# One RGCN highway layer on Trainium2: three pairs of blocks of h transposed by DMA, the edge index begun earlier on 16-bit keys

## The chip, the cores and the metric

The kernel runs on one core of a Trainium2 chip. The metric is the device time of one execution in microseconds. Before the change it was 1338.72 us (median of three runs, 1337.65 to 1338.93).

## What is computed

`x` has 1250 rows of 1024 numbers, there are 20000 edges (`src`, `dst`) of 8 types. The layer normalises the rows, lets h gather from its neighbours by type, and mixes the result with h by a gate:

```python
def _rgcn(x, edge_index, edge_type, weight, root, bias):
    msgs = x[src]
    out = x @ root + bias
    for r in range(weight.shape[0]):
        mask = (edge_type == r).astype(x.dtype)
        sums = jax.ops.segment_sum(msgs * mask[:, None], dst, num_segments=n)
        cnt = jax.ops.segment_sum(mask, dst, num_segments=n)
        mean = sums / jnp.maximum(cnt, 1.0)[:, None]
        out = out + mean @ weight[r]
    return out
...
h = jnp.maximum(_layernorm(x, axis=-1), 0.0)
u = _rgcn(h, edge_index, edge_type, weight, root, bias)
z = jnp.concatenate([u, h], axis=1) @ w_gate + b_gate
return x + jnp.tanh(u) * z + h * (1.0 - z)
```

Everything is float32; all weights are 1024x1024 (`w_gate` is two such).

## The kernel before

**Matrices and pairs.** h is multiplied with eleven 1024x1024 matrices in turn: the eight of the edge types, `root`, and the two halves of `w_gate`, the last of them with u. Matrix one is the first of them (`s == 0`). The ten blocks of 128 rows (the last has 98) are taken as five pairs, counted from zero: pair i is block i beside block i + 5. A pair times a matrix is a two-by-two scheme with seven products (Strassen-Winograd; `product`), each 128x512 by 512x512: `p1` (A11), `p5` (S1), the sixth (S2), `p3` (S4), `p7` (S3), `p2` (A12), the fourth (A22). One `lead` bank of PSUM collects several of them and is copied out by ScalarE in between, so a product that goes on adding into a bank waits for the copy before it. From matrix two on, some products are themselves divided (`First`, `Second`, `Third`).

**Where the operands come from.** For each pair `h_op[i]` holds seven operands, with h transposed: A11, A12, A21 and A22 are the transposed quarters, S1 to S4 are sums of them (`left`, on VectorE). A block of h is 128 rows by 1024; `transposed` (L366) has TensorE turn eight 128x128 pieces of it into two PSUM banks, ScalarE copies one bank out and VectorE the other. This happens once, beside matrix one: `norms` (L1220) normalises block after block (statistics on VectorE, root and relu on ScalarE), stores h and x + h to DRAM, and calls `factored` for the pair, then `left`.

**The order.** It is written by hand: each engine does its instructions in the order in which the program issues them. After each product, `between(j)` is called, one *call*; what stands beside the products is written as generators that go one step on at each call. In matrix one, pair i, these are calls 7i to 7i + 6. `index` (L1269) runs `norms` and `columns` (keys of the edges, as columns) side by side, and after both `slots`: for 40 groups of four chunks of 128 edges it works out at which place of `table` each edge goes. A group goes through a round of two calls, in several stages: one-hots on ScalarE (L1055 to L1057), counts on TensorE (L1069), sums on VectorE, a look on TensorE (L1124), place and rank on VectorE (L1132 to L1145). Keys and their low seven bits were written to DRAM as 32-bit words and are read again, broadcast over the partitions, group by group (`load_keys`, L1088). After every four rounds `to_table` issues the 16 scatters of those edges on GpSimd (L1163). `order` then sorts nodes by their number of edges. When it is done, `beside_group` (L1462) follows with `passes_over` (two small reads of maxima) and the counts.

**Queues.** SyncE (SP) issues loads of x, the stores of h and x + h (L874, L880), of the results y (L592), and the loads of keys, in program order; ScalarE issues most loads of weights; GpSimd the scatters and gathers.

**Memory.** x and its statistics live in `xpool`, which was closed with the last pair's operands, when `slots` opened its own pool in the same place.

Of the kernel before, what the change touches and what calls it, by code (L numbers as in the profile page):

```python
# [9 lines left out]
F32 = mybir.dt.float32  # L10
BF16 = mybir.dt.bfloat16
I32 = mybir.dt.int32
AF = mybir.ActivationFunctionType
# [6 lines left out]
def tile_rgcn_highway(  # L20
# [74 lines left out]
    def nedges(c):  # L95
        return P if c < NCH - 1 else EL
# [14 lines left out]
    keys_dram = dram.tile([NCH * P], I32, name="keys_dram")  # L111
    los_dram = dram.tile([NCH * P], I32, name="los_dram")
# [251 lines left out]
    def transposed(aop, part, of, n, relu=False):  # L364


        for half, to in enumerate(((A11, A12), (A21, A22))[part]):
            p = bank().rearrange("p (k f) -> p k f", k=KQ)
            for i in range(KQ):
                k = KQ * half + i  # L370
                nc.tensor.transpose(p[:, i, :n], of[:n, k * P:(k + 1) * P], ident[:n, :n])
            to_n, p_n = aop[:, to, :, :n], p[:, :, :n]
            if half and relu:
                nc.vector.tensor_scalar_max(to_n, p_n, 0.0)
            elif half:
                nc.vector.tensor_copy(to_n, p_n)
            else:
                nc.scalar.activation(to_n, p_n, AF.Relu if relu else AF.Copy)
            if n < P:
                nc.gpsimd.memset(aop[:, to, :, n:], 0.0)  # L380
# [426 lines left out]
    room = [keep.tile([P, 2, n], F32, name=f"inner{k}") for k, n in enumerate((H, H, P, P))]  # L807
    p5_room = keep.tile([P, H], F32, name="inner4")

    with ExitStack() as early:  # L810
        ix1 = early.enter_context(tc.tile_pool(name="ix1", bufs=1))


        first_part = early.enter_context(ExitStack())
        xpool = first_part.enter_context(tc.tile_pool(name="xpool", bufs=3))
# [159 lines left out]
        def columns():  # L975
# [18 lines left out]
            for to, of in ((keys_dram, key_i), (los_dram, lo_i)):  # L994
                nc.sync.dma_start(to[:P * P].rearrange("(c p) -> c p", p=P), of[:, 0, :])
                nc.sync.dma_start(to[P * P:].rearrange("(c p) -> c p", p=P), of[:C2, 1, :])
# [5 lines left out]
            for g in range(1, G):  # L1002
                less = late
                nc.vector.tensor_scalar(less, f["typ"], float(R0[g]),
                                        float((R0[g - 1] - R0[g]) * N),
                                        op0=OP.is_ge, op1=OP.mult)
                nc.vector.tensor_add(row, row, less)
            yield
# [24 lines left out]
            yield  # L1033

        def slots(ix):
# [115 lines left out]
            def to_table(c0, c1):  # L1151
# [9 lines left out]
                for c in range(c0, c1):  # L1161
                    n = nedges(c)
                    ins = nc.gpsimd.indirect_dma_start(  # L1163
                        out=table[:, :],
                        out_offset=bass.IndirectOffsetOnAxis(ap=at_i[:n, c:c + 1], axis=0),
                        in_=row_col[:n, c:c + 1], in_offset=None,
                        bounds_check=G * KEYS * SLOTS - 1, oob_is_err=False)
                    tc.declare_no_dep(ins.ins, query=no_wait, group="scatter", reason="each edge has its own slot")
                    tc.add_to_no_dep_group("scatter", ins.ins)

            load_keys(0)
            for j in range(ng + 3):
                for f, of in ((one_hots, j), (load_keys, j + 1), (as_bf16, j - 2),
# [45 lines left out]

        def norms():  # L1220
# [27 lines left out]
            left(h_op[2])  # L1248
            x4 = [load_x(4, 0)]
            yield  # L1250
            yield
# [39 lines left out]
        todo = index()  # L1291
# [15 lines left out]
    with ExitStack() as edges_part:  # L1307
# [154 lines left out]
        def beside_group():  # L1462

            yield
            passes_over()
# [343 lines left out]
```

## Time and profile before

The profile shows one execution of 1337.41 us; its span, from the first to the last instruction, is 1335.6 us.

| | us |
|---|---|
| median of the runs | 1338.72 |
| profiled execution | 1337.41 |
| its span | 1335.6 |
| TensorE busy | 1323.3 |
| VectorE busy | 956.9 |
| GpSimd busy | 568.5 |
| ScalarE busy | 372.7 |
| 72 + 8 transposes of h (L371), records of 274 and 248 ns | 9.8 |
| 157 scatters of edges (L1163), each | 1.05 |

Busy time is the time in which an engine had an instruction under way; records of TensorE overlap, so the length of one is more than its distance from the next. Each 128x512 product of four matmuls shows as eight records, two for each matmul. In a row of the order of time stand start, length, engine, line, operation, what is written and read, the shape and how many; an idle time before it and what ended it stand in brackets. A line with "q" (ACTq, SPq) is the queue of an engine issuing a DMA.

### The profile page before, as it was taken

What the parts mean: (1) busy time and instruction counts of PE and PEld (TensorE: products, weight loads), DVE (VectorE), ACT (ScalarE), POOL (GpSimd) and SP (SyncE); (2) the same over time, 40 slices, a digit from 0 to 9 for tenths busy, and PEclk for the clock granted to TensorE, in tenths of its full rate; (3) what the DMA queues carried; (4) which work ended last, traced back from release to release, by engine and by line L of the source; (5) the groups of instructions that cost most, each with busy time, mean ns of one, the idle gap of its engine ahead of it and who ended that gap; (6) DMA issues with size and microseconds to landing.
All of it is one profiled execution on the core that took longest, in us unless ns stands there. A gap on an engine that the chain in (4) does not pass through costs nothing.

```text
span 1335.6 us, 13410 instructions
## 1 busy us (share of the span) xinstructions
PE 1323.3 (99%) x4168; PEld 722.1 (54%) x4168; DVE 956.9 (72%) x1823; ACT 372.7 (28%) x794; POOL 568.5 (43%) x509
## 2 busy tenths in 40 slices
PE   9999999999999999999999999999999999999997
PEld 5444555455455545655655565565556556544443
DVE  7753755674675467448987978897778889867875
ACT  3335556465641212111121121112121112221210
POOL 0000364554657036501454546346365555615631
PEclk9999999999999999999999999999999999999999
DMA  8745476866754241143738778878788957969961
GB/s 318 270 182 175 104 124 141 191 126 109 172 160 95 88 114 53 53 148 111 254 127 319 244 253 333 290 238 268 277 273 301 347 192 243 308 251 296 340 168 59
DMA packets 104319, 270.94 MB, mean 203 GB/s; under 512 B 20100, under 2 KB 22354, under 8 KB 104112
## 3 DMA queue, kind: packets, MB, share of 16 engines
q1 hardware_dynamic: 44048, 119.85, 29.3%
q0 software_dynamic: 44064, 118.20, 27.7%
q10 hardware_dynamic: 16128, 31.98, 7.7%
q8 instruction: 33, 0.54, 0.2%
q14 instruction: 46, 0.38, 0.1%
HBM read 212.63 MB, written 75.49 MB: 216 GB/s over the span
## 4 chain that ended last, share of the span: by engine, by line
PE 85%; issue 4%; DVE 2%; DMA 2%; POOL 1%; ACT 0%; POOLq 0%; DVEq 0%; ACTq 0%
PE ps_b L406 41%; PE ps L406 17%; PE ps L219 14%; PE ps_b L219 4%; PE ps_n L406 4%; PE ps_q L219 2%; PE ps_n L219 2%; PE ps_q L406 2%; DMA w<-in_L_gnn_b_gate_dram 1%; DMA h_op<-z_dram,node 1%; POOL out_dram L746 1%; DVE row L1733 0%; DVE row L1734 0%; PE ps_q L1069 0%; PE ps_q L1124 0%
## 5 line engine op out<-in xcount | busy, mean ns | idle before, releaser
L406 PE MATMUL ps_b<-w,h_op 128*128 128x512 f32 x1464 | 659.6, 595 | 1.0 <-ACT row L489 0.8
L406 PEld LDWEIGHTS ps_b<-w,h_op 128*128 128x128 f32 x1464 | 273.6, 190 | 308.4 <-issue 297.4
L1339 POOL DMA_INDIRECT got<-y,idx x193 | 245.8, 1274 | 290.3 <-DVE u L1344 184.1
L1344 DVE SCALAR_TENSOR_TENSOR u<-got,w_of,u 128x1024 f32<-128x1024 f32 (+1 forms) x193 | 246.9, 1282 | 31.8 <-DMA got<-y,idx 29.3
L406 PE MATMUL ps<-w,h_op 128*128 128x512 f32 (+1 forms) x592 | 264.8, 589 | 0.1
L1163 POOL DMA_INDIRECT table<-row_col,at_i x157 | 165.2, 1052 | 185.5 <-DVE at_i L1159 133.0
L406 PEld LDWEIGHTS ps<-w,h_op 128*128 128x128 f32 x592 | 111.0, 190 | 119.2 <-issue 115.0
L431 DVE TENSOR_TENSOR row<-row 128x512 f32<-128x512 f32 x44 | 30.3, 690 | 79.0 <-ACT row L430 79.0
L430 ACT COPY row<-ps_b 128x512 f32<-128x512 f32 x53 | 31.1, 586 | 194.1 <-PE ps_b L406 194.1
L406 PE MATMUL ps_n<-w,h_op 128*128 128x512 f32 x176 | 80.1, 592 | 0.0
L489 ACT COPY row<-ps_b 128x512 f32<-128x512 f32 x54 | 31.7, 586 | 163.6 <-PE ps_b L406 163.4
L219 PE MATMUL ps<-w,h_op 128*128 128x256 f32 x288 | 74.5, 381 | 0.0
L219 PE MATMUL ps<-w,w 128*128 128x256 f32 x288 | 71.1, 380 | 0.0
L529 ACT COPY row<-ps_b 128x512 f32<-128x512 f32 x40 | 23.4, 585 | 162.6 <-PE ps_b L406 142.3
L219 PEld LDWEIGHTS ps<-w,h_op 128*128 128x128 f32 x288 | 54.0, 190 | 27.1 <-issue 21.6
L219 PE MATMUL ps<-inner,inner 128*128 128x256 f32 x264 | 67.8, 379 | 0.0
L219 PEld LDWEIGHTS ps<-w,w 128*128 128x128 f32 x288 | 54.6, 190 | 21.8 <-issue 15.8
L219 PEld LDWEIGHTS ps<-inner,inner 128*128 128x128 f32 x264 | 50.2, 190 | 14.5 <-issue 8.4
L1145 DVE SCALAR_TENSOR_TENSOR junk<-k_bc,key_col,before 128x128 f32<-128x128 int32 x157 | 55.0, 350 | 4.2
L406 PEld LDWEIGHTS ps_n<-w,h_op 128*128 128x128 f32 x176 | 33.4, 190 | 39.5 <-issue 39.0
L457 ACT COPY row<-ps_b 128x512 f32<-128x512 f32 x54 | 31.7, 587 | 75.9 <-PE ps_b L406 71.3
L1055 ACT ACTIVATE is_lo<-io,less_lo 128x128 bf16<-128x128 f32 x157 | 50.1, 391 | 0.7 <-DMA xh_dram<-xt 0.7
(238 smaller groups left out, 1469.5 us busy)
## 6 DMA issues: line engine op xcount, KB each, us to landing
y<-row SPq DMA_DIRECT2D x72, 512.0 KB
w<-in_L_gnn_weight_dram ACTq DMA_DIRECT2D x21, 1024.0 KB
w<-in_L_gnn_weight_dram SPq DMA_DIRECT2D x10, 1024.0 KB
k_bc<-keys_dram SPq DMA_DIRECT2D x39, 256.0 KB
l_bc<-los_dram SPq DMA_DIRECT2D x39, 256.0 KB
w<-in_L_gnn_w_gate_dram ACTq DMA_DIRECT2D x6, 1024.0 KB
h_dram<-h_op SPq DMA_DIRECT2D x9, 512.0 KB
u<-in_L_gnn_bias_dram SPq DMA_DIRECT2D x9, 512.0 KB
```

The source lines that it names most:

```text
L219: nc.tensor.matmul(p, a[:, k, :], b[:, k, :], start=(fresh and k == 0), stop=(k == 1), skip_group_check=True)
L406: nc.tensor.matmul(b[:, at], aop[:, i, k, :], w.of[i][:, k, at], start=(fresh and k == 0), stop=(k == KQ - 1), skip_group_check=True)
L430: nc.scalar.copy(d, b)
L431: nc.vector.tensor_add(c22, c if lone else c22, d)
L457: nc.scalar.copy(c11, b)
L489: nc.scalar.copy(c12, b)
L529: nc.scalar.copy(c21, b)
L1055: nc.scalar.activation(is_lo[:, i, :], io, AF.Abs, bias=less_lo[:, c0 + i:c0 + i + 1])
L1145: nc.vector.scalar_tensor_tensor(junk, o["k_bc"][:, i, :], key_col[:, c:c + 1], before, op0=OP.is_equal, op1=OP.mult, accum_out=rank[:, c: ...
L1163: ins = nc.gpsimd.indirect_dma_start(out=table[:, :], out_offset=bass.IndirectOffsetOnAxis(ap=at_i[:n, c:c + 1], axis=0), in_=row_col[:n, ...
L1339: nc.gpsimd.indirect_dma_start(out=t[:n], out_offset=None, in_=y[g][:, :], in_offset=bass.IndirectOffsetOnAxis(ap=at[:n, d, k:k + 1], axis=0),
L1344: nc.vector.scalar_tensor_tensor(u[:n], t[:n], w, u[:n], op0=OP.mult, op1=OP.add)
```

## The change

The transposes of pairs two, three and four of h leave TensorE. `in_halves` has ScalarE copy a block of h into two halves, all low 16-bit words and then all high ones; `turned` has SP issue one DMA that transposes the block of 128x2048 16-bit words; `whole_again` puts low and high words together again in `h_op`, one quarter on ScalarE and one on VectorE. `turn` does this for the two blocks of a pair, a step at a time: two steps that cut and send, two that put together. The buffers are parts of `h_op[3]` and `h_op[4]` that are not yet in use, and `room_all`, which is one tile now. Pairs zero and one stay with `transposed`.

`norms_and_index` lets `columns`, `slots` and `order` run on during `norms`, but for the calls that `norms` marks HEAVY; so the index begins eleven calls sooner. `xpool` therefore stays open, and the keys are 16 bits wide, in DRAM and in the buffers. `columns` has one more rest. Scatters of edges go into a list, of which two are issued at each rest of a round. `beside_group` waits for call one of pair two.

```diff
-    keys_dram = dram.tile([NCH * P], I32, name="keys_dram")
-    los_dram = dram.tile([NCH * P], I32, name="los_dram")
+    keys_dram = dram.tile([NCH * P], I16, name="keys_dram")
+    los_dram = dram.tile([NCH * P], I16, name="los_dram")
...
+    def in_halves(of, n, to):
+
+        if n < P:
+            nc.gpsimd.memset(to[n // 32 * 32:], 0.0)
+        nc.scalar.copy(to.bitcast(U16)[:n].rearrange("p (h c) -> p h c", h=2),
+                       of.bitcast(U16)[:n].rearrange("p (c h) -> p h c", h=2))
+
+    def turned(of, to):
+
+        nc.sync.dma_start_transpose(to.bitcast(U16).rearrange("p (c r) -> p c r", r=P),
+                                    of.bitcast(U16))
+
+    def whole_again(aop, part, of, n):
+
+        of = of.bitcast(U16).rearrange("p (h a k r) -> p h a k r", h=2, a=2, r=P)
+        for a, to in enumerate(((A11, A12), (A21, A22))[part]):
+            (nc.vector.tensor_copy if a else nc.scalar.copy)(
+                aop[:, to].bitcast(U16).rearrange("p k (r h) -> p h k r", h=2)[..., :n],
+                of[:, :, a, :, :n])
...
+    room_all = keep.tile([P, 4 * H + 4 * P], F32, name="inner")
+    room = [room_all[:, a:a + 2 * n].rearrange("p (k n) -> p k n", k=2)
+            for a, n in ((0, H), (2 * H, H), (4 * H, P), (4 * H + 2 * P, P))]
...
+        xpool = early.enter_context(tc.tile_pool(name="xpool", bufs=3))
         first_part = early.enter_context(ExitStack())
-        xpool = first_part.enter_context(tc.tile_pool(name="xpool", bufs=3))
...
-            for to, of in ((keys_dram, key_i), (los_dram, lo_i)):
+            for to, of, name in ((keys_dram, key_i, "key_h"), (los_dram, lo_i, "lo_h")):
+                half = ix0.tile([P, 2, P], I16, name=name)
+                nc.vector.tensor_copy(half, of)
+                of = half
...
+        placed = []
+
+        def scatter(count):
+
+            for c in placed[:count]:
+                n = nedges(c)
+                ins = nc.gpsimd.indirect_dma_start(
+                    out=table[:, :],
+                    out_offset=bass.IndirectOffsetOnAxis(ap=at_i[:n, c:c + 1], axis=0),
+                    in_=row_col[:n, c:c + 1], in_offset=None,
+                    bounds_check=G * KEYS * SLOTS - 1, oob_is_err=False)
+                tc.declare_no_dep(ins.ins, query=no_wait, group="scatter", reason="each edge has its own slot")
+                tc.add_to_no_dep_group("scatter", ins.ins)
+            del placed[:count]
...
                 for name, of, bufs in (("k_bc", keys_dram, 5), ("l_bc", los_dram, 3)):
-                    t = now.setdefault(j, {})[name] = ix.tile([P, CG, P], I32, name=name,
+                    t = now.setdefault(j, {})[name] = ix.tile([P, CG, P], I16, name=name,
                                                               bufs=bufs)
                     nc.sync.dma_start(t[:, :m, :].rearrange("p c e -> p (c e)"),
                                       of[None, c0 * P:(c0 + m) * P].to_broadcast([P, m * P]))
...
-                for c in range(c0, c1):
-                    n = nedges(c)
-                    ins = nc.gpsimd.indirect_dma_start(
-                        out=table[:, :],
-                        out_offset=bass.IndirectOffsetOnAxis(ap=at_i[:n, c:c + 1], axis=0),
-                        in_=row_col[:n, c:c + 1], in_offset=None,
-                        bounds_check=G * KEYS * SLOTS - 1, oob_is_err=False)
-                    tc.declare_no_dep(ins.ins, query=no_wait, group="scatter", reason="each edge has its own slot")
-                    tc.add_to_no_dep_group("scatter", ins.ins)
+                placed.extend(range(c0, c1))
...
+                        scatter(CG // 2)
                         yield
                     elif 0 <= of < ng:
                         f(of)
...
                 for _ in range(7):
+                    scatter(CG // 2)
                     yield
+                scatter(len(placed))
...
+        def turn(i, blocks, second, *of):
+
+            def flat(t):
+                return t.rearrange("p a k f -> p (a k f)")
+
+            to, of = (room_all[:, :D], flat(second)), [flat(t) for t in of]
+            for part in range(2):
+                b = blocks[part]
+                in_halves(b.ht, b.n, of[part])
+                turned(of[part], to[part])
+                yield
+            for part in range(2):
+                whole_again(h_op[i], part, to[part], blocks[part].n)
+                yield
+
         def norms():
             for _ in range(3):
                 yield
             x3 = [load_x(3, part) for part in range(2)]
             b2 = [Normed(2 + part * NP, x2[part], scratch(NP - 1, part)) for part in range(2)]
             both(*b2)
-            yield
+            for b in b1:
+                b.with_x()
+            yield
+            turn_of = turn(2, b2, h_op[3][:, 0:2], h_op[3][:, S2:S3 + 1], h_op[4][:, S2:S3 + 1])
+            next(turn_of)
             for b in b2:
                 b.store()
             yield
-            for b in b1:
-                b.with_x()
-            yield
-            factored(2, b2)
+            next(turn_of)
+            yield
             b2[0].with_x(b2[0].ht)
             b2[1].with_x()
+            x4 = [load_x(4, 0)]
+            yield
+            next(turn_of)
+            yield
+            next(turn_of)
+            yield
             left(h_op[2])
-            x4 = [load_x(4, 0)]
-            yield
             yield
             b3 = [Normed(3 + part * NP, x3[part], scratch(NP - 1, part)) for part in range(2)]
             both(*b3)
-            yield
+            yield HEAVY
+            turn_of = turn(3, b3, h_op[3][:, S1:S2 + 1], h_op[4][:, S2:S3 + 1], h_op[3][:, 0:2])
+            next(turn_of)
             for b in b3:
                 b.store()
-            yield
-            factored(3, b3)
-            left(h_op[3])
+            yield HEAVY
+            next(turn_of)
             yield
             for b in b3:
                 b.with_x()
             x4.append(load_x(4, 1))
             yield
+            next(turn_of)
+            yield
+            next(turn_of)
+            yield
+            left(h_op[3])
+            yield
+            b4 = [None, None]
+            turn_of = turn(4, b4, h_op[4][:, S1:S2 + 1], h_op[4][:, 0:2], h_op[4][:, S3:S4 + 1])
             for part in range(2):
-                ht = xpool.tile([P, D], F32, name="xt") if part else scratch(NP - 1, 1)
-                b = Normed(4 + part * NP, x4[part], ht)
+                ht = xpool.tile([P, D], F32, name="xt") if part else \
+                    h_op[4][:, S3:S4 + 1].rearrange("p a k f -> p (a k f)")
+                if part:
+                    b4[0].with_x()
+                b = b4[part] = Normed(4 + part * NP, x4[part], ht)
                 b.stats(0)
                 b.stats(1)
                 b.spread()
                 b.relu()
                 b.store()
                 yield
-                yield
-                transposed(h_op[4], part, b.ht, b.n)
-                b.with_x()
-                yield
+                next(turn_of)
+                yield HEAVY
+            b4[1].with_x()
+            next(turn_of)
+            yield
+            next(turn_of)
+            yield
             left(h_op[4])
+
+        def index():
+            yield from columns()
             first_part.close()
-
-        def index():
-            for _ in zip_longest(norms(), columns()):
-                yield
             with tc.tile_pool(name="ix", bufs=2) as ix:
                 yield from slots(ix)
             for k, t in enumerate((key_col, row_col.bitcast(F32), rank)):
                 nc.sync.dma_start(edges_dram[k], t)
             yield from order()
 
-        todo = index()
+        def norms_and_index():
+
+            later = index()
+            for heavy in norms():
+                if not heavy:
+                    next(later)
+                yield
+            yield from later
+
+        todo = norms_and_index()
         going = [True]
 
         while going[0]:
         def beside_group():
 
             yield
+            while at_call != [2, 1]:
+                yield
             passes_over()
```

More of the change, by code (lines that the diff above doesn't have):

```diff
@@ L12 @@
 I32 = mybir.dt.int32
+I16 = mybir.dt.int16
+U16 = mybir.dt.uint16
 AF = mybir.ActivationFunctionType
@@ L378, in transposed @@
                 nc.scalar.activation(to_n, p_n, AF.Relu if relu else AF.Copy)
+            if n < P:
+                nc.gpsimd.memset(aop[:, to, :, n:], 0.0)
+    def in_halves(of, n, to):
+        if n < P:
+            nc.gpsimd.memset(to[n // 32 * 32:], 0.0)
[10 more added lines that the diff above has]
+                of[:, :, a, :, :n])
             if n < P:
@@ L805, in rows_and_weights @@
                 yield
-    room = [keep.tile([P, 2, n], F32, name=f"inner{k}") for k, n in enumerate((H, H, P, P))]
+    room_all = keep.tile([P, 4 * H + 4 * P], F32, name="inner")
+    room = [room_all[:, a:a + 2 * n].rearrange("p (k n) -> p k n", k=2)
+            for a, n in ((0, H), (2 * H, H), (4 * H, P), (4 * H + 2 * P, P))]
     p5_room = keep.tile([P, H], F32, name="inner4")
@@ L1218, in order @@
                     yield
+        HEAVY = True
+        def turn(i, blocks, second, *of):
[10 more added lines that the diff above has]
+                yield
         def norms():
@@ L1241, in norms @@
             yield
-            for b in b1:
-                b.with_x()
+            next(turn_of)
             yield
-            factored(2, b2)
             b2[0].with_x(b2[0].ht)
             b2[1].with_x()
-            left(h_op[2])
             x4 = [load_x(4, 0)]
             yield
+            next(turn_of)
+            yield
+            next(turn_of)
+            yield
+            left(h_op[2])
             yield
```

## The prediction

> **What bounds the kernel now.** I read the page's busy shares first, then TensorE's order of time through matrix one, then ScalarE's, SyncE's and the busy time by stretch for the same microseconds.
>
> ```profile
> span 1335.6 us, 13410 instructions
> ...
> PE 1323.3 (99%) x4168; PEld 722.1 (54%) x4168; DVE 956.9 (72%) x1823; ACT 372.7 (28%) x794; POOL 568.5 (43%) x509
> ...
> PEclk9999999999999999999999999999999999999999
> ...
> q0 software_dynamic: 44064, 118.20, 27.7%
> ```
>
> TensorE is idle for 12.3 of 1335.6 us, and the granted clock is full in every slice. So only two things can move the time: matmul work taken off TensorE, and new waits of TensorE. Next, TensorE in order of time (start, length, instructions):
>
> ```profile
> 42.16 3.60 PE L406 MATMUL ps_b<-w,h_op 128*128 128x512 f32 x8
> ...
> 46.40 3.70 PE L406 MATMUL ps<-w,h_op 128*128 128x512 f32 x8
> 49.94 1.91 PE L371 MATMUL ps<-ident,h_op 128*128 128x128 f32 x16
> 51.69 3.60 PE L406 MATMUL ps_b<-w,h_op 128*128 128x512 f32 x8
> ...
> 65.42 1.91 PE L371 MATMUL ps<-ident,h_op 128*128 128x128 f32 x16
> 67.39 3.70 PE L406 MATMUL ps<-w,h_op 128*128 128x512 f32 x8
> ...
> 81.22 1.04 PE L371 MATMUL ps<-ident,h_op 128*128 128x128 f32 x8
> 82.10 3.60 PE L406 MATMUL ps<-w,h_op 128*128 128x512 f32 x8
> ...
> 92.40 0.84 PE L371 MATMUL ps<-ident,xt 98*128 98x98 f32 x8
> 93.08 3.62 PE L406 MATMUL ps<-w,h_op 128*128 128x512 f32 x8
> ```
>
> One product is eight records and takes 3.43 us from start to start (42.16 to 45.59). The transposes stand in this row with nothing beside them: what follows starts when they are through, so their price is the distance of starts.
>
> **The change, part by part.**
>
> *Taken off TensorE.* The transposes of pairs two, three and four (counting from zero): 51.69-49.94 = 1.75, 67.39-65.42 = 1.97, 82.10-81.22 = 0.88, 93.08-92.40 = 0.68, together **5.28 us**. Nothing is added to TensorE: its counts, looks and products are the same instructions, and the two transposes of `passes_over` stay in their place, because the new gate (pair two, call one of matrix five) is where the old order already had them. With them go six PSUM copies on ScalarE (0.60) and six on VectorE (0.69), neither of which set TensorE's pace.
>
> *Added on ScalarE.* Six deinterleaves (`in_halves`, 128x2048 of two bytes) and six of the copies of `whole_again`. The rows to price them:
>
> ```profile
> 13.16 1.06 ACT L952 ACTIVATE h_op<-h_op 128x1024 f32<-128x1024 f32 x1
> ...
> 45.08 0.57 ACT L469 COPY row<-ps 128x512 f32<-128x512 f32 x1
> 45.80 0.59 ACT L489 COPY row<-ps_b 128x512 f32<-128x512 f32 x1
> ```
>
> 512 more elements cost 1.06-0.59 = 0.47, so 2048 cost 2.47-0.47 = 2.0 us if elements count, 1.06 if bytes do; I take 2.0, since no row shows a copy faster per element. A half of `whole_again` has 1024: 1.06 on ScalarE, 1.22 on VectorE (the 128x1024 add at L879). ScalarE gains 6x2.0 + 6x1.06 - 3.6 = 14.8 us, and eleven calls of index (five and a half rounds of about 3.9 us: four absolutes 1.28, three long activations, one cast) come forward, 21 us.
>
> ```profile
> 33.00:67.00 34.00, 34.00 (x105) 16.81 (x104) 27.20 (x61) 11.06 (x18) 0.20 (x1) 1.00 0.73 272
> 67.00:100.00 33.00, 32.95 (x93) 15.39 (x91) 17.61 (x31) 10.00 (x19) 0.20 (x1) 1.00 0.48 181
> 100.00:134.00 34.00, 33.77 (x105) 15.62 (x103) 12.78 (x42) 18.30 (x46) 0.00 (x0) 1.00 0.53 178
> ```
>
> (Stretch, its length, busy time of PE, PEld, DVE, ACT, POOL, clock, DMA share, GB/s.) ScalarE is busy 39.4 of these 101 us and would be 75: it fits, but a PSUM copy now queues behind a deinterleave. TensorE needs such a copy one product, 3.43 us, after it is ready; 2.0 + 0.59 leaves 0.84. The tightest place is pair one: the first deinterleave needs the adds of `with_x`, moved up to about 46.9 on VectorE (43.9 as before, 0.58 for the two new casts of the keys, 2.35 for the adds); it ends at about 49, the copy of the sixth product at 49.6, and TensorE wants that bank at 49.8. I put **0.5 us** for all six places. If the cover is gone, the price is what a copy is late.
>
> *Added on SP: the six transposes.* Behind each in SP's queue stand the stores of h, the sums of x and h, and from pair three on the loads of keys; those who wait for them (ScalarE's `to_los`, the next `in_halves`) have a call or more. The issue is 0.32 us like any on SP. What is waited for in order is the landing: ScalarE's and VectorE's `whole_again` stop for it, with the later PSUM copies behind them. The trace has no transposing DMA. Lower bound, the same 512 KB moved plainly from SBUF, seen by a load that had to wait for a store to land:
>
> ```profile
> 54.87 0.32 SPq L880 DMA_DIRECT2D xh_dram<-xt  x1
> 57.66 0.33 SPq L824 DMA_DIRECT2D xt<-in_x_dram  x1
> ```
>
> 57.66-54.87-0.32 = 2.5 us. Upper bound: a transposed block of 128x2048 two-byte elements is 2048 runs of 256 B, 128 of them to each of 16 engines; queue q0, of which nearly half the packets are scattered words, took 0.277x16x1335.6/44064 = 134 ns a packet, so 17.2 us. I take the plain copy, the nearest row in size, source and queue, and call one landing L = **2.5 us**.
>
> Where it binds (my walk through the new order, with 3.43 a product): pair two's first transpose is issued at 49.3, two 512 KB stores go between (1.9 us each at the 272 GB/s of that stretch), so the second lands at 49.3 + L + 3.9 + L = 53.1 + 2L, if one is served after the other. Behind it come `left`, the statistics and relu of pair three and only then the copy of product five, some 10.5 us, which TensorE needs at 70.4: it must land by about 59.8, L up to 3.3. Pair three has 75.2 + 2L against 85.5, L up to 5.1; pair four has its second at 104.7 + L against 109.7, L up to 5.0. So the stall is 2(L-3.3) + 2(L-5.1) + (L-5.0), each term from its own point on: nothing at 2.5, the 5.3 us of gain eaten at L = 5.4.
>
> [...]
>
> *Index sooner, keys of 16 bits, scatters spread.* The two casts are counted above. The broadcast loads halve, 78 of 256 KB, and only relieve the queues. The rounds come 11 calls earlier, but with the same waits: two calls between what feeds a matmul and the matmul; and since a matrix has an odd number of them (50, less three left out) the old kernel ran these rounds in both phases against the products without a wait of TensorE. The 157 scatters stay 157 on POOL (1.05 us each, POOL busy 43%); two at each rest is four a round, the rate at which edges become ready, and the last seven calls of `order` take what is left, so they end some four calls earlier. No term: **0**. Cover gone (a late look holds TensorE for ScalarE's backlog of a round), 3.9 us or more.
>
> *Sum*, against the profiled execution: 1335.6 - 5.28 + 0.5 = 1330.8 span; its run was 1337.41, so 1332.6; the median of the runs is 1.31 above that run: **1333.9 us**, 0.36% less. A change under about 0.2% (2.7 us) can't be told from none.
>
> **The rivals.**
>
> *Transposes that take long.* One mechanism: L beyond 5.4, at the second transpose of each pair, TensorE waiting for S1 or for the copy of product five. For it: nothing in the trace bounds L from above but 17.2, and two must land for each pair. Against it: a plain copy lands in 2.5, and DMA is only half busy from 67 us on. At L = 7 it is 7.4 + 3.8 + 2.0 = 13.2 us of stall, 1338.7 - 5.3 + 13.2 = 1346.6; at 17.2, 64 us, 1398. Chance 0.21, nearly all of it slower.
>
> *ScalarE's backlog.* The two-byte strided copies cost 3 us rather than 2.0: the copies behind the six deinterleaves come 0.2 to 1 us late each, 1 to 6 us, so 1335 to 1339, middle 1337.5. For it: 0.84 us of margin; against it: ScalarE has idle stretches of 2 to 6 us between copies. Chance 0.14, mostly within 0.2%.
>
> *The index meets its data late.* It gives no gain in itself, and any look or count that now waits costs TensorE directly; 5 to 9 us over three matrices, 1339 to 1343. Against it: both phases ran clean before. Chance 0.05. That the transposes were hidden anyway is excluded by the distances of starts.
>
> **How the numbers follow.** The forecast has 0.60, with its own range 1332.2 (no stall, 1333.4, less the 1.28 by which the runs before spread) to 1336.0. Faster: 0.60 and 0.03 of the backlog, 0.63. Same: 0.10 of the backlog, 0.02 of long transposes, 0.12. Slower: 0.19 + 0.05 + 0.01 = 0.25. The range of 8 in 10 goes from 1332.2 up to L = 7, 1346.6.
>
> **What would show it.** No L371 transposes of pairs two to four; pair two's first product directly behind pair one's last, about 60; TensorE busy 5 us less and idle still about 12 to 13. Wrong if TensorE's idle time names a `whole_again` copy, a sum of `left` or a PSUM copy between 49 and 115 us, if a transpose lands more than 5 us after its issue, or if counts and looks of the index show waits.

## The result, and the profile after

| | before | after |
|---|---|---|
| median of nine runs each, us | 1338.72 | 1333.51 |
| lowest to highest | 1337.52 to 1339.98 | 1332.95 to 1335.19 |
| span of the profiled execution | 1335.6 | 1331.2 |
| TensorE busy / idle | 1323.3 / 12.3 | 1318.1 / 13.1 |
| ScalarE busy | 372.7 | 386.8 |

The ratio is 0.9965, with a 95% interval of 0.9956 to 0.9974: the changed kernel is faster by 5.2 us (0.35%). The forecast was 1333.9.

First the head of the page of the changed kernel, its busy shares, clock, transfers and the queue that carries the transposes (packets, MB, share of 16 engines):

```profile
span 1331.2 us, 13340 instructions
...
PE 1318.1 (99%) x4120; PEld 716.5 (54%) x4120; DVE 957.4 (72%) x1825; ACT 386.8 (29%) x800; POOL 573.4 (43%) x510
...
PEclk9999999999999999999999999999999999999999
...
DMA packets 116799, 263.72 MB, mean 198 GB/s; under 512 B 33150, under 2 KB 44818, under 8 KB 116592
...
q1 hardware_dynamic: 56528, 112.62, 28.1%
```

TensorE does 48 instructions less and is busy 5.2 us less; its idle time grew by 0.8. That is the whole balance: 1335.6 - 5.2 + 0.8 = 1331.2. Before, queue q1 had 44048 packets and there were 20100 under 512 bytes; 12480 and 13050 have come. 12480 is six times 2080, so a transposing DMA is 2080 packets, about one for each of the 2048 runs of 256 bytes counted in the prediction; with the transposes back on TensorE (first experiment) q1 has 44048 again, and three more transposing DMAs (fourth experiment) bring it to 62768.

TensorE in order of time, where the transposes stood (L430 is the product, L493 the PSUM copy of ScalarE, formerly L406 and L469):

```profile
42.20 3.60 PE L430 MATMUL ps_b<-w,h_op 128*128 128x512 f32 x8
46.15 3.70 PE L430 MATMUL ps<-w,h_op 128*128 128x512 f32 x8 [0.35 <-ACT row L493]
...
57.46 7.03 PE L430 MATMUL ps_b<-w,h_op 128*128 128x512 f32 x16
64.33 3.60 PE L430 MATMUL ps<-w,h_op 128*128 128x512 f32 x8
67.76 3.60 PE L430 MATMUL ps_b<-w,h_op 128*128 128x512 f32 x8
71.19 3.60 PE L430 MATMUL ps<-w,h_op 128*128 128x512 f32 x8
```

The row of sixteen records is the last product of pair one and the first of pair two, end to end, from about 60.9 on; no transpose stands between. Products three and five follow without a gap. The only new wait in this stretch stands in brackets: 0.35 us in pair one for the PSUM copy of product five.

SP's queue in the same time, with the issue of the transposing DMAs (L393), then ScalarE (L388 is `in_halves`, L400 `whole_again`, L513 and L493 PSUM copies):

```profile
48.62 3.55 SPq L393 DMA_TRANSPOSE inner<-h_op  x1
52.23 1.03 SPq L900 DMA_DIRECT2D h_dram<-h_op  x2
53.37 4.24 SPq L393 DMA_TRANSPOSE h_op<-h_op  x1
```

```profile
46.70 1.90 ACT L388 COPY h_op<-h_op 128x2048 uint16<-128x2048 uint16 x1 [0.60 <-ACT row L493]
48.50 0.58 ACT L513 COPY row<-ps_b 128x512 f32<-128x512 f32 x1
48.98 1.90 ACT L388 COPY h_op<-h_op 128x2048 uint16<-128x2048 uint16 x1
...
54.71 1.34 ACT L400 COPY h_op<-inner 128x1024 uint16<-128x1024 uint16 x1
59.36 1.35 ACT L400 COPY h_op<-h_op 128x1024 uint16<-128x1024 uint16 x1 [3.31 <-DMA h_op<-h_op]
...
70.45 0.56 ACT L493 COPY row<-ps 128x512 f32<-128x512 f32 x1
```

The second transpose is issued from 53.37 on, and the issue alone takes SP 4.24 us, where the two plain stores before it took 1.03 us together. ScalarE stands 3.31 us in `whole_again` until it lands: 59.36 - 53.37 = 6.0 us from the start of the issue, 59.36 - 57.61 = 1.75 from its end. The copy that TensorE needs for product five's bank ends at 71.01, and the product that needs it starts at 71.19.

VectorE at the same place (L905 is the add of `with_x`, which overwrites the buffer the store of h reads):

```profile
55.26 1.23 DVE L905 TENSOR_TENSOR h_op<-h_op,h_op 128x1024 f32<-128x1024 f32 x1 [4.62 <-DMA h_dram<-h_op]
...
61.57 0.74 DVE L400 COPY h_op<-h_op 128x1024 uint16<-128x1024 uint16 x1
...
62.41 2.75 DVE L411 TENSOR_TENSOR h_op<-h_op 128x512 f32<-128x512 f32 x4
```

The store stood behind the 3.55 us issue of the first transpose, so VectorE idled 4.62 us. It cost TensorE nothing: S1, the first of the four results of `left` at 62.41, is there at about 63.1, and the product that reads it starts at 64.33.

### The profile page after: what moved, and what is told of

The parts are those of the page before. It is cut to its first block, busy times and chain, and to the rows that moved or that the text cites. A ratio compares the mean times of both kernels' runs of the same rounds, so it can differ in the third digit from the quotient of the medians.

```text
span 1331.2 us, 13340 instructions
## 1 busy us (share of the span) xinstructions
PE 1318.1 (99%) x4120; PEld 716.5 (54%) x4120; DVE 957.4 (72%) x1825; ACT 386.8 (29%) x800; POOL 573.4 (43%) x510
## 4 chain that ended last, share of the span: by engine, by line
PE 91%; issue 3%; DMA 2%; DVE 2%; POOL 1%; SPq 1%; ACT 0%; POOLq 0%; DVEq 0%
PE ps_b L430 44%; PE ps L430 18%; PE ps L221 14%; PE ps_n L430 5%; PE ps_b L221 4%; PE ps_q L221 2%; PE ps_q L430 2%; PE ps_n L221 2%; DMA xt<-in_x_dram 1%; DMA w<-in_L_gnn_weight_dram 1%; DMA h_op<-in_L_gnn_b_gate_dram 0%; POOL out_dram L770 0%; SPq L850 0%; PE ps L373 0%; PE ps_q L1114 0%
## 5 line engine op out<-in xcount | busy, mean ns | idle before, releaser
L430 PE MATMUL ps_b<-w,h_op 128*128 128x512 f32 x1464 | 659.7, 595 | 1.0 <-ACT row L513 0.8
L430 PEld LDWEIGHTS ps_b<-w,h_op 128*128 128x128 f32 x1464 | 273.6, 190 | 308.1 <-issue 296.4
L430 PE MATMUL ps<-w,h_op 128*128 128x512 f32 (+1 forms) x592 | 264.9, 589 | 0.3 <-ACT row L493 0.3
L1071 POOL DMA_INDIRECT table<-row_col,at_i x157 | 168.6, 1074 | 135.4 <-DVE at_i L1204 52.1
L430 PEld LDWEIGHTS ps<-w,h_op 128*128 128x128 f32 x592 | 111.0, 190 | 121.4 <-issue 115.0
L430 PE MATMUL ps_n<-w,h_op 128*128 128x512 f32 x176 | 80.1, 592 | 0.0
L513 ACT COPY row<-ps_b 128x512 f32<-128x512 f32 x54 | 31.6, 586 | 162.1 <-PE ps_b L430 162.1
L221 PE MATMUL ps<-w,h_op 128*128 128x256 f32 x288 | 74.4, 381 | 0.0
L221 PE MATMUL ps<-w,w 128*128 128x256 f32 x288 | 71.1, 380 | 0.0
L221 PEld LDWEIGHTS ps<-w,h_op 128*128 128x128 f32 x288 | 54.1, 190 | 27.6 <-issue 21.6
L221 PE MATMUL ps<-inner 128*128 128x256 f32 x264 | 67.8, 379 | 0.0
L221 PEld LDWEIGHTS ps<-w,w 128*128 128x128 f32 x288 | 54.6, 190 | 21.8 <-issue 15.8
L1190 DVE SCALAR_TENSOR_TENSOR junk<-k_bc,key_col,before 128x128 f32<-128x128 int16 x157 | 55.0, 350 | 4.2
L221 PEld LDWEIGHTS ps<-inner 128*128 128x128 f32 x264 | 50.1, 190 | 14.6 <-issue 8.4
L430 PEld LDWEIGHTS ps_n<-w,h_op 128*128 128x128 f32 x176 | 33.4, 190 | 39.5 <-issue 39.2
```

The costliest lines, as they stand in the source:

```text
L221: nc.tensor.matmul(p, a[:, k, :], b[:, k, :], start=(fresh and k == 0), stop=(k == 1), skip_group_check=True)
L430: nc.tensor.matmul(b[:, at], aop[:, i, k, :], w.of[i][:, k, at], start=(fresh and k == 0), stop=(k == KQ - 1), skip_group_check=True)
L513: nc.scalar.copy(c12, b)
L1071: ins = nc.gpsimd.indirect_dma_start(out=table[:, :], out_offset=bass.IndirectOffsetOnAxis(ap=at_i[:n, c:c + 1], axis=0), in_=row_col[:n, ...
L1190: nc.vector.scalar_tensor_tensor(junk, o["k_bc"][:, i, :], key_col[:, c:c + 1], before, op0=OP.is_equal, op1=OP.mult, accum_out=rank[:, c: ...
```

## The experiments

The experiments ran in three batches, each on one chip and beside the kernel before. The first four ran on a chip where the kernel before took 1337.48 us. The others ran on a second chip where it took 1389.12 (first batch there) and 1385.50 (second batch). The traces from there, all of the changed kernel and its variants, have further waits of TensorE in the index (in the changed kernel 8.5 us in three at L221); these runs are compared only with each other and with the runs beside them.

### The transposes back on TensorE, the rest of the change kept

```diff
             for part in range(2):
                 b = blocks[part]
-                in_halves(b.ht, b.n, of[part])
-                turned(of[part], to[part])
+                transposed(h_op[i], part, b.ht, b.n)
                 yield
             for part in range(2):
-                whole_again(h_op[i], part, to[part], blocks[part].n)
                 yield
```

> The changed kernel with the transposes of pairs two to four back on TensorE; index sooner, 16-bit keys and spread scatters stay. Theory (the whole gain is the 5.28 us of transposes taken off TensorE): 1333.5 + 5.3 = 1338.8 us, the kernel before. Rival (the sooner index, the narrower keys or the spread scatters give part of it): 1337.3 or less.

Measured: 1338.80 us, ratio to before 1.0009 (1.0000 to 1.0018); TensorE busy 1323.5, span 1337.0. One wait of TensorE's table of waits is new:

```profile
PE ps L373 <- ACT h_op L895: 1.5, 1, 1.5
```

(What waits, for what, then us in total, times, longest.) A transpose waits 1.5 us for the relu of its block: it stands sooner here than in the kernel before. With the transposes back on TensorE the gain is gone, so all of it is theirs; what remains of the change costs about 1.3 us in this arrangement, and this one wait is of that size.

### The index at its old time

```diff
         def index():
-            yield from columns()
+            for _ in zip_longest(norms(), columns()):
+                yield
...
-        todo = norms_and_index()
+        todo = index()
...
             yield
-            while at_call != [2, 1]:
-                yield
             passes_over()
```

> The changed kernel with the index begun after the norms, as before, and without the gate of passes_over; DMA transposes, 16-bit keys and spread scatters stay. Theory (nothing but TensorE's transposes counts, the index is hidden either way): 1333.5 us within 1.5. Rival (the sooner index carries part of the gain): 1335.5 or more. A smaller rival (the sooner index costs ScalarE's copies something): 1332.5 or less.

Measured: 1333.08 us, ratio 0.9967 (0.9955 to 0.9979), span 1331.3. The index's eleven calls are worth nothing in either direction.

### The scatters sixteen in a row again

```diff
                     if f is None:
-                        scatter(CG // 2)
+                        scatter(len(placed))
                         yield
```

> The changed kernel with the 16 scatters of four rounds issued at once again. Theory (GpSimd is off the path): 1333.5 us within 1.5. Rival (the row of scatters holds up something of the sooner index): 1336 or more.

Measured: 1332.86 us, ratio 0.9970 (0.9957 to 0.9983), span 1331.0. Nothing, as well.

### The second transpose of each pair issued twice

```diff
                 in_halves(b.ht, b.n, of[part])
+                if part:
+                    turned(of[part], to[part])
                 turned(of[part], to[part])
```

> The changed kernel with the second DMA transpose of each pair issued twice, so that it lands some 5.5 us later (its issue takes 4.1 us, its landing 1.8 more). Theory (the second landing is where it binds, with a margin of 0.2 to 2 us): TensorE waits 3.9 us in pair two (copy of product five), 4.9 in pair three (product one waits for A11, since the copy into it must wait for the second transpose to have read its source), 3.5 in pair four (S1): 1333.5 + 12.3 = 1346 us, between 1341 and 1349. Rival (the transposes are hidden with room to spare, and the half microsecond of the forecast is all there is to lose): below 1336.

Measured: 1342.81 us, ratio 1.0044 (1.0029 to 1.0060), span 1341.4, 10.2 over the changed kernel (1331.2; the two runs before this one have 1331.3 and 1331.0 on this chip). So the landing of the second transpose does decide, once it is late enough. SP's row for pair two, and the `whole_again` that waits for it:

```profile
53.42 7.72 SPq L393 DMA_TRANSPOSE h_op<-h_op  x2
...
63.75 1.34 ACT L400 COPY h_op<-h_op 128x1024 uint16<-128x1024 uint16 x1 [7.69 <-DMA h_op<-h_op]
```

The landing is 63.75 - 59.36 = 4.39 us later than in the changed kernel. What TensorE makes of that, in its order of time, pairs two (two rows), three and four:

```profile
65.86 3.70 PE L430 MATMUL ps<-w,h_op 128*128 128x512 f32 x8 [1.37 <-DVE h_op L411]
...
73.76 3.70 PE L430 MATMUL ps<-w,h_op 128*128 128x512 f32 x8 [0.77 <-ACT row L493]
...
91.59 6.75 PE L430 MATMUL ps_b<-w,h_op 128*128 128x512 f32 x8 [3.42 <-ACT h_op L400]
...
123.54 3.70 PE L430 MATMUL ps<-w,h_op 128*128 128x512 f32 x8 [0.27 <-DVE h_op L411]
127.08 0.26 PE L1169 MATMUL ps_q<-s_b,to_lo 128*128 128x40 bf16 x4
```

Of the 4.39 us, TensorE loses two waits at pair two, 1.37 for S1 and 0.77 for the copy of product five. By starts the product behind them is 73.76 - 71.19 = 2.57 us later than in the changed kernel, so 1.8 us were margin. Pair three loses most: 3.42 us for a copy of `whole_again`, and then its product takes 6.75 us instead of 3.60. The same kernel's busy time by stretch (length; busy PE, PEld, DVE, ACT, POOL; clock; DMA share; GB/s) tells why:

```profile
87.90:91.50 3.60, 0.27 (x1) 0.00 (x0) 1.28 (x3) 1.31 (x2) 0.00 (x0) 0.92 0.74 147
91.59:98.17 6.58, 6.58 (x8) 2.65 (x9) 4.48 (x11) 6.49 (x16) 0.00 (x0) 0.53 0.84 262
98.40:105.30 6.90, 6.90 (x22) 3.12 (x19) 5.71 (x20) 5.63 (x8) 0.42 (x1) 1.00 0.72 271
```

In the stretch behind the wait the granted clock is 0.53, and full again behind that. In the changed kernel the same stretches have 1.00. Waits 1.37 + 0.77 + 3.42 + 0.27 = 5.8 and 3.15 of slow clock make 9.0 of the 10.2 us. Starts give a little more: the look in the last row starts at 117.36 in the changed kernel, so 9.7 us are lost by there, and only some 0.5 us behind it. The total came out near the theory's 12.3, its parts did not: it asked for 3.9, 4.9 and 3.5 us of waiting in pairs two, three and four, where 2.1, 3.4 and 0.3 were waited, and it had no slow product.

### Every transpose issued twice, in two batches

```diff
                 in_halves(b.ht, b.n, of[part])
                 turned(of[part], to[part])
+                turned(of[part], to[part])
                 yield
```

> The changed kernel with every one of the six DMA transposes issued twice: both of a pair land later, the second by 3.6 us more than where only the second was doubled (its landing there was at 63.8). Theory (a wait of TensorE of more than about 3.4 us is paid twice, as the granted clock falls to about half for the product behind it, as it did behind the 3.42 us wait of the run before): waits of 5.0 + 0.8 us in pair two, 7.0 in pair three, 3.9 in pair four, each of these three with 3.2 us of half clock behind it: 1333 + 26 = 1359 us. Rival (the slow product there had another cause, and a wait costs what it lasts): 1333 + 17 = 1350 us, and no stretch with a clock of 0.5 behind a wait.

> All six transposes doubled again, on the chip of the other runs. As before: theory (waits over some 3.4 us are followed by a product at about half clock) 1359 us where the changed kernel takes 1333.5; rival (a wait costs what it lasts) 1350 us.

Measured: 1404.38 us beside 1389.12 before, ratio 1.0109 (1.0075 to 1.0144); and in the next batch 1403.99, which is 22.8 us above the changed kernel of that batch. The clock reading asked for 26 and its rival for 17. The second batch lies nearer the first; in the first batch the changed kernel did not run, and with the ratio of 0.9971 measured below it would be some 19 us, nearer the rival. Each has two runs, and on this chip runs of one kernel spread by several us (1378.25 to 1384.91 for the changed kernel), so the time alone does not decide. The traces do: a wait of 5.71 us is followed by a product of 6.14, in a stretch of granted clock 0.58, and full clock behind it; and all six waits of this kind in the two traces, 3.92 to 5.94 us, are followed by products of 5.14 to 6.57.

```profile
70.13 6.14 PE L430 MATMUL ps<-w,h_op 128*128 128x512 f32 x8 [5.71 <-DVE h_op L411]
```

```profile
70.00:76.00 6.00, 5.87 (x8) 2.57 (x9) 5.18 (x13) 3.80 (x8) 0.00 (x0) 0.58 0.67 183
76.20:82.00 5.80, 5.80 (x15) 2.57 (x14) 0.19 (x2) 5.73 (x5) 0.00 (x0) 1.00 0.61 201
```

### The changed kernel again, on the second chip

> The changed kernel once more, as the measure for the other runs on this chip. Both theories: 0.9965 of the kernel before; a chip on which the kernel before itself waits elsewhere may show less.

Measured: 1381.23 us (twelve runs) beside 1385.50, ratio 0.9971 (0.9948 to 0.9995): the gain, 4.3 us, is there on the slower chip too.

### The same path for u, in the last matrix

If a transpose costs TensorE its own time and a DMA costs it nothing, the transposes of u in the last matrix should pay as well. Three pairs (twice) and four pairs were tried, cut and sent at calls 0 and 1 of the pair before theirs, put together at its calls 4 and 5; the four pairs differ only in `0 < i < NP`.

```diff
+        def by_dma(i):
+            return 0 < i < NP - 1
...
-            elif j == 3:
+            elif j == 3 and not by_dma(i):
                 for part, d, n in pair(i):
                     transposed(h_op[i % 2], part, us.pop(d), n)
...
+            if by_dma(i):
+                flat = [h_op[4][:, k:k + 2].rearrange("p a k f -> p (a k f)") for k in (0, 2, 4)]
+                of, to = flat[:2], (flat[2], room_all[:, :D])
+                if j < 2:
+                    in_halves(us[2 * i + j], nrows(2 * i + j), of[j])
+                    turned(of[j], to[j])
+                elif j in (4, 5):
+                    us.pop(2 * i + j - 4)
+                    whole_again(h_op[i % 2], j - 4, to[j - 4], nrows(2 * i + j - 4))
+                    if j == 5:
+                        left(h_op[i % 2])
```

> The changed kernel, with the same path used for u in the last matrix: pairs one to three of u are cut in halves on ScalarE at calls zero and one of the pair before, transposed by DMA, and put together at calls four and five. Theory (TensorE's own work sets the time there too): three times 1.75 us less, 1333.5 - 5.25 = 1328.2 us. Rival (the last matrix is bound by the gathers, VectorE's finishing and the scatters behind TensorE, so work taken off TensorE only becomes waiting): 1332 or more.

> As the run with three pairs of u, with pair four too (its last block has 98 rows, so two clearings on GpSimd are in the path). Theory: 1333.5 - 3 x 1.75 - 1.55 = 1326.7 us. Rival (GpSimd's clearing waits behind the gathers and scatters in its queue, ScalarE behind it, and TensorE behind ScalarE's copies): no better than with three pairs, or worse, 1328 to 1335.

> Three pairs of u by DMA again, beside the changed kernel on the same chip, as the run before fell on a chip where the kernel before took 1389 us. Theory now: it loses wherever it runs, since TensorE waited 10 and 17 us for the sums of left, which stood on VectorE behind multiplications that wait for gathers, and since one transpose's issue stretched to 20 us beside the gathers: 15 to 30 us above the changed kernel. Rival (that was this chip alone): 5 us below the changed kernel.

Measured: 1405.58 us for three pairs, ratio to before 1.0116 (1.0080 to 1.0153); 1409.65 for four, 1.0152 (1.0126 to 1.0179); three again 1401.47, 1.0146 (1.0098 to 1.0194), which is 20 us above the changed kernel beside it. It loses, where the theory asked for a gain of 5. SP's issues, TensorE's waits, and what VectorE and ScalarE stood waiting for, of three pairs in the first batch:

```profile
1246.82 6.14 SPq L393 DMA_TRANSPOSE h_op<-h_op  x1
...
1270.69 8.32 SPq L393 DMA_TRANSPOSE h_op<-h_op  x1
...
1312.11 20.64 SPq L393 DMA_TRANSPOSE inner<-h_op  x1
```

```profile
1278.35 5.97 PE L430 MATMUL ps_n<-w,h_op 128*128 128x512 f32 x8 [10.11 <-DVE h_op L411]
...
1328.10 3.70 PE L430 MATMUL ps_b<-w,h_op 128*128 128x512 f32 x8 [1.90 <-ACT h_op L400]
...
1348.89 6.54 PE L430 MATMUL ps_n<-w,h_op 128*128 128x512 f32 x8 [17.09 <-DVE h_op L411]
```

```profile
1266.59 1.23 DVE L1755 TENSOR_TENSOR h_op<-h_op,h_op 128x1024 f32<-128x1024 f32 x1 [3.40 <-DMA h_op<-z_dram,node]
```

```profile
1346.78 1.33 ACT L400 COPY h_op<-inner 128x1024 uint16<-128x1024 uint16 x1 [18.73 <-DMA inner<-h_op]
```

The long waits have two causes. The wait of 10.11 us is not for a landing: ScalarE put the second block of that pair together at 1259.67 without a wait, but `left` stands on VectorE behind multiplications that wait for gathers and starts at 1277.61. The wait of 17.09 us is for a landing: beside the gathers of this stage the same instruction takes SP up to 20.64 us to issue, and the transpose has landed at 1346.78, 34.7 us after the start of its issue. Behind the waits of 10.11 and 17.09 us the product is slow (5.97 and 6.54), behind 1.90 it is not (3.70).

### u a pair earlier

So that no sum of `left` stands behind a gather that VectorE waits for, pairs two and three of u were cut and sent at calls 5 and 6 of the pair but one before theirs, and put together at calls 0 and 1 of the pair before. That leaves two calls between the sending and the copies that wait for the landing.

```diff
+            if by_dma(i):
+                halves, whole = u_buffers()
+                if j < 2:
+                    whole_again(h_op[i % 2], j, whole[j], P)
+                    if j:
+                        left(h_op[i % 2])
+            if by_dma(i + 1) and j in (5, 6):
+                halves, whole = u_buffers()
+                in_halves(us[2 * (i + 1) + j - 5], P, halves[j - 5])
+                turned(halves[j - 5], whole[j - 5])
```

> Pairs two and three of u by DMA, sent at calls five and six of the pair but one before and put together at calls zero and one of the pair before, so that no sum stands behind a gather that VectorE waits for. Theory (work off TensorE is gain wherever the landing is not waited for): 2 x 1.75 us below the changed kernel, 1330.0 where that takes 1333.5. Rival (beside the gathers the transposes hold up SP and the gathers so long that something else waits): the changed kernel's time or above.

Measured: 1403.71 us, ratio 1.0144 (1.0094 to 1.0195), 22 us above the changed kernel beside it: a miss. TensorE's waits, the SP queue and the longest wait of ScalarE:

```profile
PE ps_b L430 <- ACT row L513: 29.8, 6, 13.1
```

```profile
1271.32 12.99 SPq L393 DMA_TRANSPOSE inner<-h_op  x1
...
1312.90 13.02 SPq L393 DMA_TRANSPOSE inner<-h_op  x1
```

```profile
1295.91 1.33 ACT L400 COPY h_op<-inner 128x1024 uint16<-128x1024 uint16 x1 [17.54 <-DMA inner<-h_op]
```

Now TensorE waits not for operands but for PSUM copies: ScalarE stands before `whole_again` until the transpose lands (1295.91, 24.6 us after the start of its issue), and L513 is queued behind it. No version faster than the changed kernel came out of this; the u runs were made on the second chip only.

## Why the prediction was right, and where it was not

**TensorE's 5.28 us.** Right: busy time fell by 5.2, and putting the transposes back takes the gain away. Reading the price from the distances of starts, not from lengths of records, gave the right size.

**The costs put at nothing.** Right for the index and the scatters, each shown by its own run (ratios 0.9967 and 0.9970, against 0.9965 with all of the change). For the counts and looks, the table of waits of the changed kernel on the first chip has no line of theirs. The casts to 16-bit keys and the added rest of `columns` are another matter: they make the new wait of the next paragraph. The keys were not tried alone.

**The 0.5 us of stall.** Right in size, but by luck: the mechanism was another. The prediction had a PSUM copy late behind a deinterleave, tightest at the copy of the sixth product in pair one. That copy did stand behind the deinterleave, from 48.50 to 49.08, and TensorE did not wait for it, nor for a copy behind any other deinterleave. The wait of 0.35 us is for the copy of product five, which comes before the first deinterleave. First the kernel before, where the key transposes stood between two products, then VectorE, ScalarE and TensorE of the changed kernel (L1022 is a cast of the keys, L895 a relu, L1043 a key transpose):

```profile
45.59 0.27 PE L1013 MATMUL ps<-ident,key 128*128 128x128 f32 x1
```

```profile
39.75 0.29 DVE L1022 CAST key_h<-key_i 128x256 int16<-128x256 int32 x1
```

```profile
44.38 1.24 ACT L895 ACTIVATE h_op<-xt,less,rs 128x1024 f32<-128x1024 f32 x1 [0.42 <-DVE less L879]
45.53 0.57 ACT L493 COPY row<-ps 128x512 f32<-128x512 f32 x1
```

```profile
49.68 0.27 PE L1043 MATMUL ps<-ident,key 128*128 128x128 f32 x1
```

Two of the costs put at nothing meet here, as the order of time shows. The two casts on VectorE hold up the statistics, with them the relu and the copy behind it, which starts at 45.53 instead of 45.08. And the key transposes, which before covered that copy from 45.59 to 46.40, come a product later by the added rest of `columns`, so the copy's delay lies open. The run with the index late has the casts, the rest and the same 0.35 us; the run with the transposes on TensorE has the casts and the rest, but a transpose stands before that product, and no such wait. Neither was taken out alone. Of the rest of the 0.8 us of idle time 0.4 is at a transpose's wait for the normalised block (L888, 1.2 against 0.8), which runs of nearly the same code have at 0.5 (the changed kernel again, second chip) to 1.2 (four pairs of u). `in_halves` took 1.90 (put at 2.0), ScalarE's part of `whole_again` 1.34 (put at 1.06), VectorE's 0.75 (put at 1.22); ScalarE gained 14.1 us (put at 14.8).

**The landing L = 2.5 us.** Mis-sized: it is 6.0, 5.8 and 6.2 us for the second transposes of the three pairs. Here are the later two, SP's issue and the `whole_again` that ends the wait:

```profile
77.49 4.06 SPq L393 DMA_TRANSPOSE h_op<-h_op  x1
...
103.94 4.08 SPq L393 DMA_TRANSPOSE h_op<-h_op  x1
```

```profile
83.27 1.34 ACT L400 COPY h_op<-inner 128x1024 uint16<-128x1024 uint16 x1 [4.22 <-DMA h_op<-h_op]
...
110.16 1.11 ACT L400 COPY h_op<-h_op 128x784 uint16<-128x784 uint16 x1 [3.27 <-DMA h_op<-h_op]
```

Two thirds of it is the issue, put at 0.32 us "like any on SP"; what comes after the issue is 1.7 to 2.1 us, and for that part the plain copy was a fair row. At L = 6 the prediction's formula asks for 2(6.0-3.3) + 2(6.0-5.1) + 1.0 = 8.2 us of stall, and TensorE had none at these places. So the formula failed too: it served the transfers one after another, 53.1 + 2L, which is 65.1, and the landing came at 59.36. In the trace the time is set by SP issuing, 3.55 + 1.03 + 4.24 us back to back, with the earlier transfers done meanwhile: the copy that reads the first transpose starts without a wait at 54.71, and the add that waits for the store at 55.26, both before the second issue ends at 57.61. Two errors of opposite sign met; the forecast of no further stall was right by luck. One of the prediction's own signs of being wrong came true, a landing more than 5 us after the issue, counted from the start of the issue; the time held all the same.

**Where it would bind.** The landing at pair two, 59.36, came 0.4 us before the deadline of 59.8 that the prediction had worked out, and the true deadline is later. VectorE, which had idled for the store of h and has other work first, reaches its half of the second `whole_again` only at 61.57, 2.2 us after the landing, and the doubled run shows 1.8 us of margin in all (4.39 against 2.57), if the delay past the margin reaches TensorE one for one, as the prediction had it; that was not shown by itself. At pair three the tightest point was another than named: the first `whole_again` writes A11 and A12 of `h_op[3]`, which the second transpose reads, so at 83.27 it waits for the second transpose and not for its own. A11 is there at 83.27 + 1.34 = 84.6, about 0.6 us ahead of the product that reads it, some 3.4 us after the start of the row at 81.81. That is where the doubled transpose cost most; the prediction's margin there was 85.5 - 80.2 = 5.3 us.

**The rivals.** The long transposes are a true mechanism, shown by the doubled ones (10.2 us over the changed kernel with the second of each pair twice), and didn't happen here because the landing stays just under the point. Their price was wrong as well: it had no slow clock behind a wait. ScalarE's backlog did not occur: the deinterleaves took 1.90 us, not 3. The index meeting its data late is excluded by the waits on the first chip. On the second chip the looks of the changed kernel do wait (5.25 and 5.34 us at L1169), and no trace of the kernel before was kept there, so whether the sooner index adds to that is not shown.

**TensorE or DMA.** With TensorE busy 99% of the span, transposes of h kept on it would have given 5.2 us away. For u they were the better ones in all three arrangements tried, where the DMA lost some 20 us.

## What to carry to other kernels

A transpose on TensorE, busy 99% of the span here, cost the distance between starts: 5.28 us by the starts, 5.2 by the busy time. A DMA in its place cost TensorE nothing where its landing, issue included, came before the first PSUM copy or operand behind it, and with the second of each pair issued twice the time rose by 10.2 us; measure that landing in the stage where it is to run, since it was 6 us in one stage and up to 35 in another. Before adding a wait, list what stands behind it on ScalarE and on SP: the store of h stood behind an issue of 3.55 us, and VectorE idled 4.62 for it; PSUM copies stood behind a `whole_again` that waited 17.54 us for its landing, and TensorE waited up to 13.1 for one of them. Waits of TensorE of 0.77 to 1.90 us ahead of a product cost themselves alone here; of the longer ones shown, 3.42 to 17.09 us, all but one (3.53) were paid again in a product of 5.14 to 6.75 us instead of 3.60.

## What was not expected of the hardware

**The clock fell behind waits.** Waits of TensorE of 0.77, 1.37 and 1.90 us were followed by products of 3.70 us; waits of 3.42, 5.71 and 10.11 us by products of 6.75, 6.14 and 5.97, at granted clocks of 0.53 to 0.61, and one product later TensorE was at its pace again (3.68, 3.60 and 3.60 us; the clock 1.00 where it was read, from 98.40 and from 76.20 on). So a wait of 3.42 us cost 3.42 + 3.15. The length of one wait does not decide alone. Nine waits of 5.60 to 17.09 us ahead of a product, in the doubled runs and the u runs, were followed by products of 5.14 to 6.58 us, but between 3.4 and 4.0 it went either way: behind 3.42 the product took 6.75, and in the three pairs of u, behind 3.53, it took 3.70.

```profile
407.28 3.70 PE L430 MATMUL ps_b<-w,h_op 128*128 128x512 f32 x8 [3.53 <-ACT row L481]
```

What decides in that range was not tried.

**The issue of a transposing DMA.** 512 KB took SP 2.1 to 4.2 us to issue beside the norms of the changed kernel, and 2.1 to 20.6 us beside gathers. What sets it was not isolated: the 2080 packets of each are the same in both stages (12480 more in q1 for the six of h, and 12480 more again for the six of u).
